# Linear attention, then a Mamba chain: GpSimd's share of the step product made uneven, its output sum, statistics, denominator and step products moved

## The chip, the cores and the metric

The kernel runs on one core of a Trainium2 chip. The core has TensorE (PE in the profile; PEld is its weight load), VectorE (DVE), ScalarE (ACT), GpSimd (POOL) and SyncE (SP, which only issues DMAs here). They run side by side and wait for each other by semaphores. The metric is the device time of one execution in microseconds, as the median of several runs.

## The reference

The input x has 8 samples of 512 channels and 2304 positions. Layer 0 is a group norm followed by causal linear attention with 8 heads, added to x. Layer 1 is a group norm followed by a chain of four Mamba blocks of 128 channels, each fed with the result of the one before, added to x again.

```python
q, k = elu(Wq x)+1, elu(Wk x)+1
den = 1 / (einsum(q, cumsum(k)) + 1e-10)
out = causal(q, k, v) * den
...
# Mamba block: 256 inner channels, 16 states
delta = softplus(dt @ Wdt.T + bdt)
dA  = exp(delta * A)               # decay
dBu = delta * xs * B               # step product
h_t = dA_t * h_{t-1} + dBu_t       # scan along the positions
y   = sum over states (C * h) + xs * D
...
fused = w_local * x_i + w_global * max(x_i, x_m)   # goes into the next block
```

## The kernel before, in words

**Chunks, slots and passes.** A *chunk* is 384 positions of one Mamba block of one sample. A block has 6 chunks, which is one *pass*; 8 samples of 4 blocks make 32 passes and 192 chunks. Two samples (two `Stream`s) take turns, pass by pass. The 256 x 16 states of a chunk are laid out as 8 *slots* (`SLOTS`); a slot has 4 groups of 128 partitions and 384 positions. The loop `slot(k)` runs over 1536 slots, and it writes out by hand the order of work on every engine.

**One slot.** GpSimd multiplies B by delta times x for the last `TAIL` = 152 columns of each group (`last_product`, L879), and VectorE does so for the other 232 columns from a copy `Bp` of B in PSUM that ScalarE makes (`inputs` L863, `product` L890). GpSimd's part is put into the queue two slots ahead, VectorE's part one slot ahead; in slot 7 VectorE does the products of both slots 0 and 1 of the next chunk. ScalarE computes the decay factors into PSUM banks (L900). VectorE runs four scans (L910). GpSimd multiplies the states by C (`weigh`, L923), and TensorE sums them over the states into `yp` (`gather`, L937), which is queued a slot and a half later: `waiting` holds up to two gathers and one is taken out in the middle of each slot. Five buffers `u` hold the states of a slot.

**Beside the slots.** Each half slot, `beside` steps a list of generators: `chunk` (the attention of a later sample), `Job.prepare` (projection, convolution, Silu L758 to L763, step sizes: two matmuls L782 and Softplus L793, then dx L834 on GpSimd), `pass_on` (mixes a block's result into the next block's input, and adds the result to x on GpSimd for the output, L696) and `statistics` (group-norm statistics of a later sample's input, L253). A generator yields when it wants its next step: a pair of the half slot and the least distance to its step before, or a distance alone as text ("1"), and with it how many free PSUM banks it needs. Six banks (`BANKS`) are shared by the decay factors and all these steps. `first` is the half slot at which a chunk begins.

**Statistics.** A sample has 24 pieces of 384 positions. Before, they are taken one per `PERIOD` (16 half slots, one chunk), by both samples of a pair in the same 24 chunks or nearly so: two in a chunk for a while, and then none.

**The denominator.** `den` is a product of `pr` with a selector (L405); VectorE adds 1e-10 (L433), takes the reciprocal (L434), and ScalarE spreads it (L441). TensorE turns it (L445), VectorE multiplies q with it (L450).

**Group norms and the end of a pass.** The attention's input norm is applied by GpSimd in four steps per chunk (L324) of each sample's first pass; the second norm's statistics end with a group norm on VectorE (L190 to L211), once a pass. At the end of a pass VectorE computes the two mixing weights: L587, an exponential on ScalarE, L593 (adds 1 to two numbers) and L594 (their reciprocal).

Of the kernel before, what the change touches and what calls it, by code (L numbers as in the profile page):

```python
# [9 lines left out]
F32 = mybir.dt.float32  # L10
# [7 lines left out]
P = 128  # L18
T = 128
LC = 384  # L20
NI, NQ, NGR = 4, 4, 4
SLOTS = 8
TAIL = 152
BANKS = 6
DEPTH = 3
LEAD = 11
# [2 lines left out]
BEFORE, PERIOD, DENSE, FIRST = 61, 16, 11, -115  # L29
# [20 lines left out]
def attention_then_mamba_kernel(  # L50
# [12 lines left out]
    nc = tc.nc  # L63
    B, _, L = x.shape
    NS = 16
    NC = L // LC
    assert L % LC == 0 and LC % T == 0

    cpool = ctx.enter_context(tc.tile_pool(name="consts", bufs=1))
# [6 lines left out]
    psx = ctx.enter_context(tc.tile_pool(name="psx", bufs=1, space=PSUM))  # L76
# [4 lines left out]
    ident = cst[:, C_ID : C_ID + P]  # L81
# [4 lines left out]
    hsel = cst[:, C_SEL : C_SEL + 2]  # L86
# [28 lines left out]
    def load_scales():  # L115
# [3 lines left out]
        nc.scalar.activation(w_a, w_a, AF.Exp)  # L119
        nc.scalar.mul(w_a, w_a, -1.0)  # L120

    power = cpool.tile([P, 4], F32, name="power")
    nc.gpsimd.memset(power, -0.5)

# [100 lines left out]
    def statistics(b):  # L225

        xv = x[b].rearrange("(t p) l -> p t l", p=P)
        stats = small.tile([P, 4, NC, 6], F32, tag="stats_a", name=f"stats_a{b}", bufs=2)
        if b == 0:

            xs = []

            def load(c):
                t = mpool.tile([P, 4, 1 + LC], F32, tag="u", name=f"xs_{c}", bufs=5)[:, :, 0:LC]
                nc.sync.dma_start(out=t, in_=xv[:, :, c * LC : (c + 1) * LC])
                xs.append(t)

            for c in range(5):
                load(c)
            load_projections()  # L240
            for c in range(NC):
                for ct in range(4):
                    nc.vector.bn_stats(stats[:, ct, c, :], xs[c][:, ct, :])
                if c == 0:
                    load(5)
                    fetch(0)
        else:
            when = begins[b] + b % 2
            for i in range(4 * NC):
                yield (when - 4, 1) if b > 1 else "1", 0  # L250
                xs = piece(b, i)
                yield (when, 1) if b > 1 else "1", 0
                nc.vector.bn_stats(stats[:, i // NC, i % NC, :], xs)  # L253
                when += PERIOD
        norms[b] = yield from group_norm(stats, 4, f"a{b}", 2)

    def piece(b, i):
# [22 lines left out]
    def chunk(m):  # L280


        b, o, c = parts[m]
        n = f"{b}_{o}_{c}"
        bank = Banks()
        NT = LC // T
        cols, tile_rows = slice(c * LC, (c + 1) * LC), slice(o * P, (o + 1) * P)
        subs = [slice(i * T, (i + 1) * T) for i in range(NT)]
# [96 lines left out]
        pr = new("pr")  # L385
# [15 lines left out]
        yield at(12), 1  # L401
        both = bank()
        den = both[:, 0 : 2 * NT]
        for i in range(NT):
            nc.tensor.matmul(den[:, 2 * i : 2 * i + 2], pr[:, subs[i]], hsel, start=True, stop=True)  # L405
        more = NT if c + 1 < NC else NT - 1
        ds = both[:, LC - NT * 64 : LC].rearrange("p (i d) -> p i d", i=NT)
        place = range(NT + 1) if c % 2 == 0 else range(NT, -1, -1)
# [2 lines left out]
        if c:  # L411
# [4 lines left out]
                start=True,  # L416
                stop=False,
                skip_group_check=True,
            )
        for i in range(more):  # L420
            for j in range(i + 1):
                for h in heads_of:
# [4 lines left out]
                        start=c == 0 and j == 0,  # L427
                        stop=j == i,
                        skip_group_check=True,
                    )  # L430
        yield at(14), 0
        rd = small.tile([P, 2 * NT], F32, tag="rd", name=f"rd_{n}", bufs=1)
        nc.vector.tensor_scalar_add(rd, den, 1e-10)  # L433
        nc.vector.reciprocal(rd, rd)  # L434
        while read[0] < m:
            yield "1w", 0
        nc.scalar.copy(S[:, kept_states, :], ds[:, 0:more, :])
# [84 lines left out]
    class Stream:  # L522
# [55 lines left out]
        def pass_on(self):  # L578
# [78 lines left out]
            for c in range(NC):  # L657

                cols, icols = slice(c * LC, (c + 1) * LC), slice(3 + c * LC, 3 + (c + 1) * LC)
                if now is None:  # L660
                    first = 2 * self.jobs[self.block * NC + c].start
                    yield (first - 30, 1), 0
                    now = loads(c)
                    yield (first - 25, 1), 0 if old is None else 1
                else:
                    yield "1", 0 if old is None else 1
                fu, xb, xa = now
                now = None
                if not last:
                    normed = dict(bias=norm[:, 1, :], scale=norm[:, 0, :])  # L670
                if old is None:
                    nc.scalar.activation(xi[:, icols], xb, AF.Identity, **normed)
                else:
                    bank = Banks()
                    mixed = bank()[:, 0:LC]
                    more = len(factors) == 3
                    for i, src in enumerate((xi[:, icols], fu)):
                        nc.tensor.matmul(  # L678
                            mixed, mix[:, i, :], src, start=i == 0, stop=i == 1, skip_group_check=True
                        )  # L680
                    yield "1", 0
                    nc.scalar.copy(fu, mixed)
                    if more:
                        nc.tensor.matmul(
                            mixed, mix[:, 2, :], xb, start=False, stop=True, skip_group_check=True
                        )
                    yield "1", 0
                    if more:
                        nc.scalar.activation(
                            xi[:, icols], mixed, AF.Identity, bias=norm[:, 1, :]  # L690
                        )
                    elif not last:
                        nc.scalar.activation(xi[:, icols], xb, AF.Identity, **normed)
                    bank.free()
                    self.ready = c + 1
                    nc.gpsimd.tensor_tensor(xa, xa, fu, ALU.add)  # L696
                    save(out[old[0], old[1] * P : (old[1] + 1) * P, cols], xa)
                self.ready = c + 1
                if last and c + 1 < NC:
                    yield "3", 0  # L700
                    now = loads(c + 1)

    class Job:
# [6 lines left out]
        def prepare(self):  # L710
# [64 lines left out]
            bank.free()  # L775
            scr = dpool.tile([2 * NS, LC], F32, tag="scr", name=f"scr_{n}")
            save(scr, dbc[0 : 2 * NS, :])
            yield "1", 2
            vps = []
            for h in range(2):  # L780
                vp = bank()[:, 0:LC]
# [1 line left out]
                    vp, steps_w[32:41, s, h * P : (h + 1) * P], dbc[32:41, :], start=True, stop=True  # L783
                )
                vps.append(vp)
            while spreading:
                yield "1w", 0
            spreading.append(n)
            yield "1", 0
            delta = mpool.tile([P, 2, LC], F32, tag="delta", name=f"delta_{n}", bufs=1)  # L790
            ahead(DEPTH + 2)
            for h in range(2):
# [66 lines left out]

        def inputs(self, pair):  # L860

            self.Bp = psx.tile([P, 2, LC - TAIL], F32, tag="Bp", name=f"Bp_{self.n}_{pair}")
            nc.scalar.copy(self.Bp, self.B[pair % 2][:, :, 0 : LC - TAIL])  # L863

        def skip(self, h):

# [4 lines left out]

        def last_product(self, s):

            shape, cols = [P, NGR, TAIL], slice(LC - TAIL, LC)
            h, q = s // NQ, s % NQ
            u = mpool.tile([P, NGR, 1 + LC], F32, tag="u", name=f"u_{self.n}_{s}", bufs=5)
            if self.c:
                nc.scalar.copy(u[:, :, 0], self.state[:, h, q, :])
            nc.gpsimd.tensor_tensor(  # L879
                u[:, :, 1 + LC - TAIL :],  # L880
                self.B[q // 2][:, q % 2, cols].unsqueeze(1).to_broadcast(shape),
                self.dxr[h][:, :, cols],
                ALU.mult,
            )
            return u

        def product(self, s, u):

            shape, cols = [P, NGR, LC - TAIL], slice(0, LC - TAIL)
            nc.vector.tensor_mul(  # L890
                u[:, :, 1 : 1 + LC - TAIL],
                self.Bp[:, s % 2, :].unsqueeze(1).to_broadcast(shape),
                self.dxr[s // NQ][:, :, cols],
            )
# [156 lines left out]
    for b in counted:  # L1051
        first = times[parts.index((b, 0, 0))]
        begins[b] = (first - 20) // PERIOD * PERIOD - 4 * NC * PERIOD - 2 if b > 1 else first - 64

    def begin(latest):

# [19 lines left out]
    def beside(half):  # L1076

        half_no[0] = half
        flush(every=False)
        begin(half // 2 + LEAD)  # L1080

        for t in heads:
            if t.need is not None and t.early() and t.fits() and t.due():
                t.step()
        held = False
        for t in tasks + heads:
            while t.need is not None and t.due():
                if not t.fits() or held and t.need[1]:
                    held = held or t.need[1] > len(spare)
                    break  # L1090
                t.step()
        prune()
# [64 lines left out]
    def slot(k):  # L1157
# [6 lines left out]
        if s == 2 and before is not None and not before.closed:  # L1164
            before.gated(1)
            tasks.insert(0, Task(finale(before)))
        elif s == 6:
            job.gated(0)
        beside(2 * k)
        for i in range(4):  # L1170
            job.scan(s, i, us[k], decays.pop(0))
# [140 lines left out]
```

## Time and profile before

| what | value |
|---|---|
| median of 3 runs | 8173.76 us (8166.18 to 8179.68) |
| profiled execution | 8173.45 us, its span 8171.6 us |
| granted TensorE clock, mean | 0.945 |
| VectorE idle, all in all | 345.8 us, of it some 140 ahead of the first scan at 196.1 us |
| GpSimd idle | 424.3 us |
| HBM | 1318.23 MB read, 327.68 MB written |

The busy share of each engine is its busy time over the span. A line of a group gives the source line, the engine, the operation, what it writes and reads, the count, the busy time, the mean duration and the idle time of the engine just ahead of it with what ended that. A line of the order of time gives the start, the duration (of a row of equal instructions, their whole stretch), the engine, the line and the operation; in square brackets stands the idle time ahead of it and what ended it. Instructions that follow each other on VectorE overlap a little in these records: four scans of 935 ns take 3.49 us together.

### The profile page before, as it was taken

The page shows a single profiled execution, that of the slowest core. Times are in us where ns is not written, and L with a number is a line of the kernel's source. Part 1 is how long each engine was busy: PE and PEld are TensorE (multiplying, and loading weights), DVE is VectorE, ACT ScalarE, POOL GpSimd, SP SyncE. Part 2 cuts the span into 40 slices and gives each one's busy share as a digit, 9 for nine tenths or more (in the row PEclk, how much of TensorE's full clock was granted, in tenths as well). Part 3 has the DMA queues.
Part 4 walks back from the last instruction along what each step waited for, and adds up shares of the span by engine and source line. Part 5 has one row for each costly group of instructions (what it writes and reads, how often), then busy time and mean ns, then how long its engine had stood idle before and what let it go on. Part 6 is the DMA issues. An engine that isn't in the chain of part 4 may idle for free. (4 is left out here: it accounts for less than half of the span.)

```text
span 8171.6 us, 133449 instructions
## 1 busy us (share of the span) xinstructions
PE 7371.7 (90%) x39882; PEld 3532.8 (43%) x39882; DVE 7825.8 (96%) x10534; ACT 6974.3 (85%) x14914; POOL 7747.3 (95%) x3905
## 2 busy tenths in 40 slices
PE   8889999998899999999899999999988999999975
PEld 5444444444444444444444444444444444444421
DVE  3999999999999999999999999999999999999998
ACT  3888888888888888888888888888888888888876
POOL 2999999999999999999999999999999999999999
PEclk9999999999999999999999999999999999999977
DMA  6778888877787788887787788887877777777765
GB/s 199 191 189 207 210 209 212 212 199 210 200 209 204 205 212 212 207 210 201 205 216 205 200 208 209 214 211 195 212 204 204 204 204 200 204 203 199 193 172 148
DMA packets 1097351, 1655.02 MB, mean 203 GB/s; under 512 B 143913, under 2 KB 989353, under 8 KB 1096498
## 3 DMA queue, kind: packets, MB, share of 16 engines
q1 hardware_dynamic: 1096626, 1646.48, 77.8%
q8 instruction: 317, 5.19, 0.3%
q14 instruction: 408, 3.34, 0.1%
HBM read 1318.23 MB, written 327.68 MB: 201 GB/s over the span
## 5 line engine op out<-in xcount | busy, mean ns | idle before, releaser
L910 DVE TENSOR_TENSOR_SCAN u<-bank,u 128x385 f32<-128x385 f32 (+1 forms) x6144 | 5435.3, 935 | 101.6 <-ACT bank L900 101.1
L923 POOL TENSOR_TENSOR u<-u,C 128x1536 f32<-128x1536 f32 x1536 | 4894.4, 3187 | 245.4 <-DVE u L910 164.3
L900 ACT ACTIVATE bank<-dr,scales 128x385 f32<-128x385 f32 (+1 forms) x6144 | 3422.3, 579 | 617.5 <-DVE u L910 573.9
L879 POOL TENSOR_TENSOR u<-B,dxr 128x608 f32<-128x608 f32 x1536 | 2285.6, 1488 | 14.8 <-DMA B<-scr 14.8
L300 PE MATMUL bank<-xn,wq 128*128 128x384 f32 x4608 | 1862.0, 552 | 262.4 <-DVE u L910 215.6
L890 DVE TENSOR_TENSOR u<-Bp,dxr 128x928 f32<-128x928 f32 x1536 | 1682.9, 1096 | 14.9 <-DMA dxr<-xscr 7.7
L937 PE MATMUL yp<-u,cst 128*32 128x384 f32 x12288 | 1357.6, 514 | 259.7 <-POOL u L923 147.7
L300 PEld LDWEIGHTS bank<-xn,wq 128*128 128x128 f32 x4608 | 939.9, 212 | 1153.2 <-DVE u L910 360.5
L722 PE MATMUL bank<-xi,wk 128*128 128x384 f32 x3072 | 1102.4, 502 | 14.5 <-ACT xr L508 13.7
L722 PEld LDWEIGHTS bank<-xi,wk 128*128 128x128 f32 x3072 | 556.2, 191 | 568.2 <-ACT bank L900 77.3
L937 PEld LDWEIGHTS yp<-u,cst 128*32 128x32 f32 x12288 | 249.3, 109 | 904.3 <-issue 412.7
L312 ACT ACTIVATE ex<-bank,bqkv_sb 128x384 f32<-128x384 f32 x384 | 221.1, 576 | 337.0 <-PE bank L300 336.1
L900 ACT ACT_TABLE_LOAD x382 | 490.1, 1283 | 6.9
L863 ACT COPY Bp<-B 128x464 f32<-128x464 f32 x768 | 419.6, 546 | 25.7 <-DMA B<-scr 12.4
L834 POOL TENSOR_TENSOR dx<-delta,xs 128x384 f32<-128x384 f32 x384 | 385.9, 1005 | 21.6 <-ACT delta L793 21.6
L733 PE MATMUL bank<-xi,scales 128*128 128x384 f32 x768 | 325.4, 510 | 50.3 <-ACT xs L758 50.3
L955 PE MATMUL bank<-yz,scales 128*128 128x384 f32 x768 | 328.1, 534 | 37.7 <-DVE yz L949 32.8
L782 PE MATMUL bank<-dbc,steps_w 9*128 9x384 f32 x768 | 306.0, 518 | 21.8 <-DVE rd L433 12.3
L769 PE MATMUL bank<-xs,scales 128*40 128x384 f32 x768 | 285.0, 494 | 0.0
L498 PE MATMUL bank<-sm,v 128*64 128x128 f32 x2304 | 255.2, 300 | 0.0
L793 ACT ACT_TABLE_LOAD x192 | 246.3, 1283 | 3.5
L758 ACT ACT_TABLE_LOAD x192 | 246.3, 1283 | 3.5
(123 smaller groups left out, 8101.2 us busy)
## 6 DMA issues: line engine op xcount, KB each, us to landing
dr<-dscr SPq DMA_DIRECT2D x1536, 192.0 KB, 4.2
dxr<-xscr SPq DMA_DIRECT2D x1536, 192.0 KB, 4.9
xn<-xn SPq DMA_DIRECT2D x192, 768.0 KB, 5.4
B<-scr SPq DMA_DIRECT2D x1536, 96.0 KB, 4.2
C<-scr SPq DMA_DIRECT2D x1536, 96.0 KB, 2.7
dscr<-delta SPq DMA_DIRECT2D x192, 384.0 KB, 5.2
xscr<-dx SPq DMA_DIRECT2D x192, 384.0 KB, 2.9
xn<-in_x SPq DMA_DIRECT2D x48, 768.0 KB, 5.3
```

What stands on the lines that cost most here:

```text
L300: nc.tensor.matmul(ps, wqs[m // NC][:, kt, j * P : (j + 1) * P], xn[:, kt, :], start=(kt == 0), stop=(kt == 3),)
L722: nc.tensor.matmul(xc, wk[:, k, h * P : (h + 1) * P], xi[:, c0 + k : c0 + k + LC], start=(k == 0), stop=(k == 3),)
L733: nc.tensor.matmul(zp, w_gate[:, s, h * P : (h + 1) * P], xi[:, c0 + 3 : c0 + 3 + LC], start=True, stop=True,)
L834: nc.gpsimd.tensor_tensor(dx[:, h, :], delta[:, h, :], xs[:, h, :], ALU.mult)
L863: nc.scalar.copy(self.Bp, self.B[pair % 2][:, :, 0 : LC - TAIL])
L879: nc.gpsimd.tensor_tensor(u[:, :, 1 + LC - TAIL :], self.B[q // 2][:, q % 2, cols].unsqueeze(1).to_broadcast(shape), self.dxr[h][:, :, col ...
L890: nc.vector.tensor_mul(u[:, :, 1 : 1 + LC - TAIL], self.Bp[:, s % 2, :].unsqueeze(1).to_broadcast(shape), self.dxr[s // NQ][:, :, cols],)
L900: nc.scalar.activation(dA[:, cols], self.dr[h][:, g, cols], AF.Exp, scale=w_a[:, self.w[1], NGR * h + g, q : q + 1],)
L910: nc.vector.tensor_tensor_scan(u[:, g, cols], dA[:, cols], u[:, g, cols], 0.0, ALU.mult, ALU.add,)
L923: nc.gpsimd.tensor_tensor(u[:, :, 0:LC], u[:, :, 1:], self.C[q // 2][:, q % 2, :].unsqueeze(1).to_broadcast([P, NGR, LC]), ALU.mult,)
L937: nc.tensor.matmul(self.yp[g * 32 : g * 32 + 32, 0:LC], state_sum, u[:, g, 0:LC], start=False, stop=s % NQ == NQ - 1, skip_group_check=True,)
L955: nc.tensor.matmul(self.xm[:, 0:LC], w_out[:, self.w[1], h, :], self.yz[:, h, :], start=(h == 0), stop=(h == 1),)
```

## The change

GpSimd's share of a step product becomes 128 columns in slots 0 and 1 of a chunk (`WIDE`) and 165 in slots 2 to 7 (`TAIL`); `Bp` takes the other 256 or 219. For samples 4 and later a piece of statistics is taken every second period, beginning earlier, so that a pair of samples takes one a chunk. The denominator's 1e-10 is added by TensorE, which starts the accumulation with a product of the unit matrix and a constant tile. The GpSimd add of the output (L696) waits for half slot `first - 17`, the second half of slot 7 of the chunk before the one ahead. The two step matmuls (L782) are issued in the step of Softplus, half a slot later than before. And in slot 1 the gather of slot 7 of the chunk before is issued at the slot's start and not in its middle.

In the order of the queues this reads so. On VectorE only the widths, the missing add and the places of the statistics differ. On GpSimd the output add stands between the last product with B and the last product with C of a chunk. On ScalarE the order is the same. On TensorE the gather of slot 7 now stands ahead of the step matmuls, and a small matmul ahead of `den`.

```diff
-TAIL = 152
+WIDE, TAIL = 128, 165
...
+    tiny = cpool.tile([P, 2 * LC // T], F32, name="tiny")
+    nc.gpsimd.memset(tiny, 1e-10)
...
-            when = begins[b] + b % 2
+            when, gap = begins[b] + (b % 2 if b < 4 else 0), PERIOD if b < 4 else 2 * PERIOD
...
-                when += PERIOD
+                when += gap
...
+        nc.tensor.matmul(den, ident, tiny, start=True, stop=False, skip_group_check=True)
         for i in range(NT):
-            nc.tensor.matmul(den[:, 2 * i : 2 * i + 2], pr[:, subs[i]], hsel, start=True, stop=True)
+            nc.tensor.matmul(
+                den[:, 2 * i : 2 * i + 2],
+                pr[:, subs[i]],
+                hsel,
+                start=False,
+                stop=True,
+                skip_group_check=True,
+            )
...
-        nc.vector.tensor_scalar_add(rd, den, 1e-10)
-        nc.vector.reciprocal(rd, rd)
+        nc.vector.reciprocal(rd, den)
...
+                    yield (first - 17, 1) if not last else "1", 0
                     nc.gpsimd.tensor_tensor(xa, xa, fu, ALU.add)
...
             save(scr, dbc[0 : 2 * NS, :])
-            yield "1", 2
+            while spreading:
+                yield "1w", 0
+            spreading.append(n)
+            yield "2", 2
             vps = []
...
                 vps.append(vp)
-            while spreading:
-                yield "1w", 0
-            spreading.append(n)
-            yield "1", 0
             delta = mpool.tile([P, 2, LC], F32, tag="delta", name=f"delta_{n}", bufs=1)
...
-            self.Bp = psx.tile([P, 2, LC - TAIL], F32, tag="Bp", name=f"Bp_{self.n}_{pair}")
-            nc.scalar.copy(self.Bp, self.B[pair % 2][:, :, 0 : LC - TAIL])
+            width = LC - (TAIL if pair else WIDE)
+            Bp = psx.tile([P, 512], F32, tag="Bp", name=f"Bp_{self.n}_{pair}")
+            self.Bp = Bp[:, 0 : 2 * width].rearrange("p (f l) -> p f l", f=2)
+            nc.scalar.copy(self.Bp, self.B[pair % 2][:, :, 0:width])
...
+            tail = TAIL if s > 1 else WIDE
+            shape, cols = [P, NGR, tail], slice(LC - tail, LC)
...
+            width = LC - (TAIL if s > 1 else WIDE)
+            shape, cols = [P, NGR, width], slice(0, width)
...
         begins[b] = (first - 20) // PERIOD * PERIOD - 4 * NC * PERIOD - 2 if b > 1 else first - 64
+        if b > 3:
+            begins[b] -= (4 * NC - b % 2) * PERIOD
...
+        if s == 1 and len(waiting) > 1:
+            waiting.pop(0)()
         beside(2 * k)
```

## The prediction on record

> **What bounds the kernel now.** I read the table of busy time first, then the groups, then the waits of VectorE, then the order of time inside one chunk (eight slots).
>
> ```profile
> PE 7371.7 (90%) x39882; PEld 3532.8 (43%) x39882; DVE 7825.8 (96%) x10534; ACT 6974.3 (85%) x14914; POOL 7747.3 (95%) x3905
> ...
> L910 DVE TENSOR_TENSOR_SCAN u<-bank,u 128x385 f32<-128x385 f32 (+1 forms) x6144 | 5435.3, 935 | 101.6 <-ACT bank L900 101.1
> L923 POOL TENSOR_TENSOR u<-u,C 128x1536 f32<-128x1536 f32 x1536 | 4894.4, 3187 | 245.4 <-DVE u L910 164.3
> L879 POOL TENSOR_TENSOR u<-B,dxr 128x608 f32<-128x608 f32 x1536 | 2285.6, 1488 | 14.8 <-DMA B<-scr 14.8
> L890 DVE TENSOR_TENSOR u<-Bp,dxr 128x928 f32<-128x928 f32 x1536 | 1682.9, 1096 | 14.9 <-DMA dxr<-xscr 7.7
> ```
>
> VectorE and GpSimd are both full; a scan waits for its decay factor (L900) 131 times, 101 us. Where that wait lies shows in the order of time, at the end of a chunk (VectorE, then ScalarE, then GpSimd):
>
> ```profile
> 2521.35 1.09 DVE L890 TENSOR_TENSOR u<-Bp,dxr 128x928 f32<-128x928 f32 x1
> 2522.37 1.79 DVE L910 TENSOR_TENSOR_SCAN u<-bank,u 128x385 f32<-128x385 f32 x2
> 2524.09 1.09 DVE L890 TENSOR_TENSOR u<-Bp,dxr 128x928 f32<-128x928 f32 x1
> 2525.10 0.54 DVE L512 BATCH_NORM_STATS2 stats_m<-xr 128x6 f32<-128x384 f32 x1
> 2525.57 0.93 DVE L910 TENSOR_TENSOR_SCAN u<-bank,u 128x385 f32<-128x385 f32 x1
> 2527.37 2.66 DVE L910 TENSOR_TENSOR_SCAN u<-bank,u 128x385 f32<-128x385 f32 x3 [0.87 <-ACT bank L900]
> ```
> ```profile
> 2521.47 0.59 ACT L900 ACTIVATE bank<-dr,scales 128x385 f32<-128x385 f32 x1 [0.27 <-DVE u L910]
> 2522.07 1.28 ACT L758 ACT_TABLE_LOAD   x1
> ...
> 2526.75 1.09 ACT L900 ACTIVATE bank<-dr,scales 128x385 f32<-128x385 f32 x2
> ```
> ```profile
> 2526.08 1.48 POOL L879 TENSOR_TENSOR u<-B,dxr 128x608 f32<-128x608 f32 x1
> 2528.47 3.17 POOL L923 TENSOR_TENSOR u<-u,C 128x1536 f32<-128x1536 f32 x1 [0.91 <-DVE u L910]
> ```
>
> In slot 7 ScalarE does the four Silu with two table loads; the last scan of the slot can't start before 2527.37, about 6.0 us after slot 6 ended (2521.35). In those 6.0 us VectorE idles 0.87 and GpSimd, held up by the late scan, 0.91. Everywhere else in this chunk VectorE runs back to back. Counting the scan starts by 32 gives each chunk's length: 53 of 192 last 40.4 us, whether they hold no statistic, one (wait 0.41) or two (wait 0): statistics lie in the hole and are free. So a chunk is a fixed window of 6.0 plus 34.4 us of VectorE work.
>
> **Part by part.** *The shares.* Slots 2 to 7 move 13 columns times 4 groups from VectorE to GpSimd. VectorE's price per element, from L890 (928: 1096 ns) and the 384-element product L386 (541 ns), is 555/544 = 1.02 ns: 52 elements are 53 ns, six products 0.32 us. All six lie in the 34.4 us, on the path. Slots 0 and 1 move 24 columns back: 96 elements, 98 ns each; both products lie in the window (2521.35 and 2524.09), where 0.87 us of waiting (0.41 with one statistic) covers them; without that cover they cost 0.2. GpSimd: L923 against its 384-element product (3187, 1005 ns) gives 1.89 ns an element, L879 against the same 2.16; so +0.10 to 0.11 in six slots, -0.18 to -0.21 in two: +0.23 us a chunk. Its chunk is 40.4 minus 0.9 idle, 39.5 of work, then 39.7.
>
> *The denominator.* VectorE loses the add L433: 141 ns and 30 ns to the dependent step, 0.17 us on the path. The reciprocal now reads PSUM. The Trainium skill (Perfetto Trace Analysis, Optimizing Scalar/DVE Operations) puts access at about 60 ns on SBUF and 125 on PSUM, which would leave 0.10. The rows: L433 read PSUM in 141 ns, L434 SBUF in 192, so PSUM isn't dearer here. I take 0.17; the rule would cost 144 x 0.07 = 10 us. Below nothing it can't go. TensorE gains a small matmul; the nearest row, L405, takes 0.83 us for six records, so 0.28 for two. The reciprocal has 0.8 us of slack after L423.
>
> *Output sum.* GpSimd's add L696 (1.0 us, 186 times) moves from slot 4 to just ahead of slot 7's product with C, into the 0.91 us hole. Nothing but that product is queued right behind it; the gather and the next chunk wait for that. Its store moves along on SP, past the loads of the next chunk's rows; only the buffer's next use, two chunks on, waits for it. With it there GpSimd has 0.1 to 0.2 us left (39.7 against 39.9).
>
> *Gather and step products.* The gather of slot 7 goes half a slot forward, ahead of the two step products (L782). Now L782 (1.55 us) runs 2529.86 to 2531.42, then the gather at 2531.70, when GpSimd lets it. Afterwards: gather to 2532.55, L782 to 2534.1. Softplus (L793) starts at 2534.70 after a table load that waits for nothing: 0.6 us of cover. Behind L782 stands the q projection L300 (2533.93 now, 1.38 of it waiting for a bank): 0.15 later. Price nothing, unless the product with C is late: then each us beyond 0.6 is ScalarE's.
>
> *Statistics.* One a chunk in the window instead of two or none: free either way; it keeps the cover above open from sample 4 on. For about 20 chunks with two (samples 2, 3) the two wider products cost 0.2.
>
> **Sum.** A free chunk (no normalization, no group norm in it) gains 0.32 + 0.17 = 0.49; the next bounds (GpSimd 39.7, TensorE's last 0.1) let me take 0.46. Of 192 chunks, 36 carry the attention's normalization on GpSimd (four L324 more): GpSimd is the bound there and they lose 0.23, as do 8 at the end: +10. Of the rest 24 hold a group norm and have TensorE without a gap from the projection on: gain 0. About 20 gain 0.29 (-6), 100 gain 0.46 (-46): -52 + 10 = -42. One stretch is still missing:
>
> ```profile
> 2461.72 3.19 POOL L923 TENSOR_TENSOR u<-u,C 128x1536 f32<-128x1536 f32 x1
> 2464.85 1.01 POOL L834 TENSOR_TENSOR dx<-delta,xs 128x384 f32<-128x384 f32 x1
> ```
> ```profile
> 2464.56 0.38 DVE L593 TENSOR_SCALAR wt<-wt 128x2 f32<-128x2 f32 x1
> ```
> ```profile
> 2464.97 0.17 DVE L594 RECIPROCAL wt<-wt 128x2 f32<-128x2 f32 x1
> ```
>
> L593, once a pass, adds 1 to two numbers; it ends with GpSimd's running instruction (2464.91). The median is 382 ns, but 5 of 32 took 2.8 to 5.8 us: they waited through that instruction and two or three behind it, until GpSimd stood idle. The change brings VectorE here 0.33 us earlier (add and three products) and GpSimd 0.3 later (three longer products): L593 meets the product 1.0 us before its end. The Trainium skill (SBUF — State Buffer, Who interferes with whom) says whoever starts first holds the shared port pair for the whole instruction: 0.65 us more, and for some 21 passes 14 us. The five rows speak for more: to GpSimd's idle moment, 3.4 us, so 3.0 more and 63 us in all. I take the rule's value, as 26 of the other waits ended with the first instruction, but not confidently: those met it 0.4 us or less before its end. Below nothing is excluded: L593 isn't removed.
>
> Forecast: -42 + 14 = -28 from the profiled execution's 8173.45 (span 8171.6; median of the runs 8173.76, the same): 8145.
>
> **Rivals.** *The port (slower).* L593 is held to the idle moment at 21 passes: -42 + 63 = +21, 8194. For: one met the product 0.9 us ahead of its end and took 3.31. Against: 26 didn't. It decides from about 2.0 us a pass on. *TensorE or GpSimd becomes the bound.* TensorE idles only 2.1 to 3.9 us a chunk, and some 1.6 is a fixed wait for the gather; with 0.28 more work and the steps behind the gather, free chunks gain 0.2 instead of 0.46: -26 off the 100, so 8145 + 26 = 8171. *All of it, and the port costs nothing* (L593 meets a gap): 8131, and 8120 if the group-norm chunks gain 0.46 too.
>
> **How the numbers follow.** Forecast 0.38, full gain 0.15, new bound 0.17, port 0.30. A measurement tells about 0.2%, 16 us. Forecast and full gain are faster: 0.53; new bound and a fifth of the port's chance are within: 0.23; the rest of the port's is slower: 0.24. The range runs from the full gain with the GpSimd-bound chunks' loss taken away (8110) to the port's case with a few passes more (8202).
>
> **What would show it.** Right: free chunks of 39.95 us; the slot-7 wait 0.67 without a statistic, 0.2 with one; L890 near 1043 and 1194 ns; L879 near 1590 and 1300; no POOL wait of 0.9 ahead of slot 7's product; L593's mean near 1.5 us. Wrong: L593 near 3.4 us (port), free chunks at 40.2 with L793 or L300 waiting behind L782 (new bound), or a scan waiting for L900 in slot 2, where it has 0.3 us to spare.

## The result and the profile after

The changed kernel takes 8202.53 us (median of 5 runs, 8191.29 to 8213.21) against 8169.36 us (8162.39 to 8179.68) for the kernel before on the same chip: 1.0039 times as long, 95% interval 1.0028 to 1.0051. That is 33 us slower, where 28 us less was forecast. The profiled execution has a span of 8196.9 us (before 8171.6), at a mean granted clock of 0.943 (before 0.945).

The page's busy times and the four groups shown before, after the change (L910 is now L923, L923 is L936, L879 is L891, L890 is L903):

```profile
PE 7431.8 (91%) x40266; PEld 3598.0 (44%) x40266; DVE 7798.2 (95%) x10342; ACT 6950.1 (85%) x14914; POOL 7802.0 (95%) x3906
...
L923 DVE TENSOR_TENSOR_SCAN u<-bank,u 128x385 f32<-128x385 f32 (+1 forms) x6144 | 5435.6, 935 | 125.9 <-ACT bank L913 75.4
L936 POOL TENSOR_TENSOR u<-u,C 128x1536 f32<-128x1536 f32 x1536 | 4896.0, 3188 | 204.6 <-DVE u L923 107.7
...
L891 POOL TENSOR_TENSOR u<-B,dxr 128x660 f32<-128x660 f32 (+1 forms) x1536 | 2341.6, 1524 | 22.2 <-DMA B<-scr 21.9
...
L903 DVE TENSOR_TENSOR u<-Bp,dxr 128x876 f32<-128x876 f32 (+1 forms) x1536 | 1659.3, 1080 | 14.1 <-ACT Bp L874 7.2
```

VectorE is busy 27.6 us less and GpSimd 54.7 us more, and the scans' wait for the decay factor fell from 101.1 to 75.4 us. So the work moved as planned, and yet the end came later. The end of a chunk looks as forecast too. VectorE, in order of time, at slot 7 of one chunk, then GpSimd:

```profile
2535.03 0.54 DVE L521 BATCH_NORM_STATS2 stats_m<-xr 128x6 f32<-128x384 f32 x1
2535.49 0.93 DVE L923 TENSOR_TENSOR_SCAN u<-bank,u 128x385 f32<-128x385 f32 x1
2536.64 2.66 DVE L923 TENSOR_TENSOR_SCAN u<-bank,u 128x385 f32<-128x385 f32 x3 [0.21 <-ACT bank L913]
```
```profile
2537.74 3.18 POOL L936 TENSOR_TENSOR u<-u,C 128x1536 f32<-128x1536 f32 x1
```

The wait is 0.21 us with one statistic (forecast 0.2), and GpSimd no longer idles ahead of slot 7's product with C. Free chunks last 39.89 us (forecast 39.95; before 40.41).

One wait that grew is one that the forecast did not touch: VectorE's multiplication of q with the transposed reciprocal. The line gives the total, the number of times and the longest wait; first before, then after:

```profile
DVE q L450 <- PE bank L445: 44.5, 59, 5.9
```
```profile
DVE q L459 <- PE bank L454: 87.9, 94, 4.4
```

A second wait is as large and stands under another name. Scans of slot 2 waited 52 times in the 184 chunks between the two ends, 47.8 us in all, and never before the change. The profile puts most of that down to GpSimd, as in the first line below. But each of these scans starts within 0.2 us of the end of its own decay factor (L913), which ScalarE computes behind Softplus; and Softplus and its table load (both L802) now wait for the step products (L795), which they never did before:

```profile
DVE u L923 <- POOL u L891: 19.9, 28, 2.1
```
```profile
ACT delta L802 <- PE bank L795: 53.9, 74, 2.0
ACT L802 <- PE bank L795: 31.3, 30, 3.2
```

On TensorE the wait of the gathers for GpSimd's product with C grew likewise, before and after:

```profile
PE yp L937 <- POOL u L923: 147.7, 185, 5.3
```
```profile
PE yp L950 <- POOL u L936: 391.8, 204, 4.8
```

TensorE's order of time in two chunks of the changed kernel shows what happens. In the first one the granted clock stays at 1.00:

```profile
2501.09 0.85 PE L950 MATMUL yp<-u,cst 128*32 128x384 f32 x8 [1.55 <-POOL u L936]
2501.87 1.55 PE L795 MATMUL bank<-dbc,steps_w 9*128 9x384 f32 x4
2503.35 2.85 PE L302 MATMUL bank<-xn,wq 128*128 128x384 f32 x8
2506.04 0.49 PE L454 MATMUL bank<-cst,rdb 128*128 128x128 f32 x3
```

VectorE comes to L459 only at 2508.61, two microseconds after L454 is done. In the next chunk the same four rows run like this, and VectorE's row stands behind them:

```profile
2540.98 0.85 PE L950 MATMUL yp<-u,cst 128*32 128x384 f32 x8 [1.55 <-POOL u L936]
2541.76 2.31 PE L795 MATMUL bank<-dbc,steps_w 9*128 9x384 f32 x4
2544.01 5.43 PE L302 MATMUL bank<-xn,wq 128*128 128x384 f32 x8
2549.27 0.49 PE L454 MATMUL bank<-cst,rdb 128*128 128x128 f32 x3
```
```profile
2549.80 0.55 DVE L459 TENSOR_TENSOR q<-q,bank 128x384 f32<-128x384 f32 x1 [1.21 <-PE bank L454]
```

The table by stretches of that chunk (stretch, length, busy time and count of PE, PEld, DVE, ACT, POOL, then PEclk, DMA share, GB/s) names the reason in its PEclk column:

```profile
2537.50:2540.90 3.40, 1.92 (x34) 0.94 (x32) 3.40 (x6) 3.40 (x10) 3.30 (x3) 1.00 0.66 186
...
2542.50:2549.30 6.80, 6.80 (x12) 3.12 (x11) 6.09 (x8) 5.23 (x10) 6.80 (x3) 0.50 1.05 293
```

For 6.8 us TensorE gets half its clock. The step products and the q projection, 4.40 us together in the first chunk, take 7.74.

The mean clock of the page hides this, for the records of the clock show it in many chunks and mostly in this place, for one or two pieces of 3.413 us: of the 120 stretches at half clock in the middle 184 chunks, 82 begin 3 to 6 us after slot 0 does. The kernel before has it too. I counted, in each kernel's one trace, the chunks (of 184, without those at the two ends) that hold at least two such pieces in their first 20 us, and call them *half-clock chunks* (such a count shifts by up to four with where the borders are drawn):

| kernel | half-clock chunks | their median | median of chunks with none |
|---|---|---|---|
| before | 79 | 41.35 us | 40.41 us |
| changed | 84 | 42.00 us | 39.89 us |

A chunk without it gained 0.52; one with it lost 0.65.

### The profile page after: what moved, and what is told of

It is laid out like the page before. It is cut to its first block, busy times and chain, and to the rows that moved or that the text cites. A ratio compares the mean times of both kernels' runs of the same rounds, so it can differ in the third digit from the quotient of the medians.

```text
span 8196.9 us, 133855 instructions
## 1 busy us (share of the span) xinstructions
PE 7431.8 (91%) x40266; PEld 3598.0 (44%) x40266; DVE 7798.2 (95%) x10342; ACT 6950.1 (85%) x14914; POOL 7802.0 (95%) x3906
## 5 line engine op out<-in xcount | busy, mean ns | idle before, releaser
L923 DVE TENSOR_TENSOR_SCAN u<-bank,u 128x385 f32<-128x385 f32 (+1 forms) x6144 | 5435.6, 935 | 125.9 <-ACT bank L913 75.4
L936 POOL TENSOR_TENSOR u<-u,C 128x1536 f32<-128x1536 f32 x1536 | 4896.0, 3188 | 204.6 <-DVE u L923 107.7
L913 ACT ACTIVATE bank<-dr,scales 128x385 f32<-128x385 f32 (+1 forms) x6144 | 3411.0, 579 | 544.5 <-DVE u L923 512.7
L891 POOL TENSOR_TENSOR u<-B,dxr 128x660 f32<-128x660 f32 (+1 forms) x1536 | 2341.6, 1524 | 22.2 <-DMA B<-scr 21.9
L903 DVE TENSOR_TENSOR u<-Bp,dxr 128x876 f32<-128x876 f32 (+1 forms) x1536 | 1659.3, 1080 | 14.1 <-ACT Bp L874 7.2
L874 ACT COPY Bp<-B 128x438 f32<-128x438 f32 (+1 forms) x768 | 414.9, 540 | 30.2 <-DVE u L903 15.9
L795 PE MATMUL bank<-dbc,steps_w 9*128 9x384 f32 x768 | 400.0, 653 | 1.9 <-ACT S L446 1.9
L795 PEld LDWEIGHTS bank<-dbc,steps_w 9*128 9x128 f32 x768 | 159.2, 228 | 212.4 <-ACT bank L913 99.3
```

The costliest lines, as they stand in the source:

```text
L795: nc.tensor.matmul(vp, steps_w[32:41, s, h * P : (h + 1) * P], dbc[32:41, :], start=True, stop=True)
L874: nc.scalar.copy(self.Bp, self.B[pair % 2][:, :, 0:width])
L891: nc.gpsimd.tensor_tensor(u[:, :, 1 + LC - tail :], self.B[q // 2][:, q % 2, cols].unsqueeze(1).to_broadcast(shape), self.dxr[h][:, :, col ...
L903: nc.vector.tensor_mul(u[:, :, 1 : 1 + width], self.Bp[:, s % 2, :].unsqueeze(1).to_broadcast(shape), self.dxr[s // NQ][:, :, cols],)
L913: nc.scalar.activation(dA[:, cols], self.dr[h][:, g, cols], AF.Exp, scale=w_a[:, self.w[1], NGR * h + g, q : q + 1],)
L923: nc.vector.tensor_tensor_scan(u[:, g, cols], dA[:, cols], u[:, g, cols], 0.0, ALU.mult, ALU.add,)
```

## The experiments

Ratios are to the kernel before on the same chip, with their 95% intervals.

**The order put back.** The first two tell whether TensorE's order is the cause.

```diff
-            while spreading:
-                yield "1w", 0
-            spreading.append(n)
-            yield "2", 2
+            yield "1", 2
             vps = []
...
+            while spreading:
+                yield "1w", 0
+            spreading.append(n)
+            yield "1", 0
             delta = ...
...
-        if s == 1 and len(waiting) > 1:
-            waiting.pop(0)()
         beside(2 * k)
```

> The changed kernel with the step products and the gather of slot 7 put back where they were (nothing else undone). Theory (TensorE's order): where the granted clock falls to 0.5 just as the late gather, the step products and the q projection follow each other, they take about twice as long and VectorE waits 1.2 us for the transposed reciprocal; undone, the chunks with such a dip come back from 42.0 to about 41.0 us, free chunks stay at 39.9, and the whole is 8135 to 8155. Rival (GpSimd's longer shares are the bound): nothing changes, 8195 to 8205. Rival (the port, L593): nothing changes either.

Measured: 8134.12 us (0.9956, 0.9944 to 0.9969). The order alone made 68 us of difference. Its trace has 60 half-clock chunks with a median of 41.14 us, and no scan of slot 2 waits. By the page's span and busy time VectorE idles 329.5 us, against 398.7 in the changed kernel. I compared the two traces chunk by chunk: the 53 chunks that hold two pieces at half clock only with the order of the change are 79 us longer there, and the 36 that hold none in either trace are not longer (6 us shorter in all). VectorE's wait, and TensorE's rows in one half-clock chunk (line numbers differ by a few: L792 are the step products, L951 the gather):

```profile
DVE q L459 <- PE bank L454: 49.7, 52, 4.4
```
```profile
2434.29 1.55 PE L792 MATMUL bank<-dbc,steps_w 9*128 9x384 f32 x4
2436.19 0.85 PE L951 MATMUL yp<-u,cst 128*32 128x384 f32 x8 [0.35 <-POOL u L937]
2437.87 5.49 PE L302 MATMUL bank<-xn,wq 128*128 128x384 f32 x8 [0.82 <-DVE u L924]
2443.15 0.85 PE L454 MATMUL bank<-cst,rdb 128*128 128x128 f32 x3
```
```profile
2444.04 0.56 DVE L459 TENSOR_TENSOR q<-q,bank 128x384 f32<-128x384 f32 x1 [0.54 <-PE bank L454]
```

Here the step products run at full clock while GpSimd still works on slot 7; only the q projection meets the half clock, and it starts 5.4 us into the chunk where it was 6.5 in the changed kernel. VectorE waits 0.54 us and not 1.21. Either half of this edit alone leaves TensorE's order as it was before: the step products and the gather only change places if both are moved.

**The order alone,** put into the kernel before (the same edit, the other way round).

> The kernel before with only the step products half a slot later and the gather of slot 7 ahead of them. Theory (TensorE's order): free chunks stay at 40.4 us, chunks with a clock dip at the end go from 41.5 to about 42.3, the whole 8210 to 8235. Rival (GpSimd's shares or the port): as before, 8165 to 8175.

Measured: 8205.56 us (1.0043, 1.0029 to 1.0057), 35 us slower; 84 half-clock chunks with a median of 42.29 us, free chunks unchanged at 40.41. The theory holds a little below its numbers. The rivals fall.

**The shares put back** (`WIDE, TAIL = 152, 152` in the changed kernel).

> The changed kernel with GpSimd's share back at 152 columns in all slots. Theory (TensorE's order): the loss stays and the gain of 0.32 us a free chunk goes, 8205 to 8230. Rival (GpSimd is the bound with its 0.23 us more a chunk): 8170 or less. Rival (the port): VectorE comes 0.3 us later and GpSimd 0.3 earlier to L593, whose mean goes back to 0.8 us: 10 us less of the loss, 8190.

Measured: 8193.26 us (1.0028, 1.0016 to 1.0039), within the intervals the same as the changed kernel. The number is the port rival's, and L602's mean did fall to 0.75 us; L602 takes 14.6 us less in all, which is worth some 10 us if each of them costs 0.7, as a later run finds for the changed kernel (an estimate: 27 for 38.7). The theory missed its range: free chunks are 0.33 us longer (40.22), as it said, but this trace also has fewer half-clock chunks (72 and not 84), and the scans of slot 2 wait 26.2 us and not 47.8. What each of these three is worth was not separated. GpSimd was not the bound.

**The add put back** (the small matmul out, `tensor_scalar_add` in).

> The changed kernel with the small matmul taken out and the add of 1e-10 back on VectorE. Theory (TensorE's order with a slow clock): VectorE does 0.17 us more in the free chunks, TensorE 0.28 less, but half a chunk away from the queue that is late: 8205 to 8220. Rival (TensorE's extra work in the normalization is what makes it late and pulls the clock down): 8180 or less, with fewer stretches at half clock than 134.

Measured: 8231.21 us (1.0075, 1.0062 to 1.0088), beyond both: more half-clock chunks (99), not fewer. TensorE's added matmul is not what slows it.

**Half of the q projection left out,** with the order of the change.

```diff
-            for kt in range(4):
+            steps = 4 if j else 2
+            for kt in range(steps):
```

> The changed kernel, with the order of the change kept, but the q projection of each attention chunk leaves out half of its sum (two of four matmuls). Theory (TensorE is late only because it does the late gather, the step products and the q projection one after another, at half clock in many chunks): with 1.4 us (2.7 at half clock) less in that row, the transposed reciprocal is in time again, the chunks with a dip come down from 42.0 to 41.2 us or less and the whole to 8110 to 8160. Rival (what the new order makes late is ScalarE's Softplus or the banks, not TensorE's own time): 8185 to 8205.

Measured: 8138.01 us (0.9961, 0.9948 to 0.9973). VectorE's wait for the transposed reciprocal is all but gone:

```profile
DVE q L460 <- PE bank L455: 6.4, 4, 3.1
```

So TensorE's own time in that row is what came late there. The rival holds for the other wait: the scans of slot 2, behind Softplus, still wait 59.0 us. At the same time the clock was worse (0.928, 94 half-clock chunks): less work made more half clock.

**The add of 1 as a sum of two tensors,** from here on with the order put back, to take away the hold of L602.

```diff
-                nc.vector.tensor_scalar_add(wt[:, 0:2], wt[:, 0:2], 1.0)
+                nc.vector.tensor_tensor(wt[:, 0:2], wt[:, 0:2], ones, ALU.add)
```

> The kernel of the first experiment (the order put back, all else of the change kept), with the add of 1 to two numbers (L602) done as an addition of two tensors on the same engine at the same place. In the first experiment its 32 calls took 51.8 us in all. Theory (they wait for the port that GpSimd holds, and that wait is on VectorE's path): they take about 0.1 us each, and the whole falls by 25 to 48 us from 8134, to 8086 to 8109. Rival (the wait is covered by what comes late behind it anyway, or the addition of two tensors waits too): 8125 to 8140.

Measured: 8138.68 us (0.9965, 0.9951 to 0.9979). It took nothing away: this form waited just as long, 51.6 us in all against 51.8. The lines give least, median and longest of the 32 calls in ns; before, the changed kernel, and this one (L604):

```profile
L593 DVE TENSOR_SCALAR wt<-wt x32: 169/382/5765, 462.9 to 8157.6; 128x2 f32<-128x2 f32 x32
```
```profile
L602 DVE TENSOR_SCALAR wt<-wt x32: 169/934/4130, 464.4 to 8182.6; 128x2 f32<-128x2 f32 x32
```
```profile
L604 DVE TENSOR_TENSOR wt<-wt,ones x32: 160/1074/5927, 455.4 to 8114.8; 128x2 f32<-128x2 f32 x32
```

The Trainium skill (SBUF — State Buffer, Who interferes with whom) has the reason: a VectorE instruction with two inputs in SBUF also meets GpSimd's reads, and this one has two. L903, which runs beside GpSimd throughout, has one of its inputs in PSUM.

**The shares put back, the order put back.**

> The kernel of the first experiment (the order put back), with GpSimd's share back at 152 columns in all slots. Theory (the shares gain 0.32 us in free chunks, cost 0.2 in those that GpSimd bounds, and bring L602 later into GpSimd's product, 51.8 us in all against about 24): free chunks 40.3, the whole 8128 to 8150. Rival (the shares gain their 0.32 us nearly everywhere and the port costs nothing): 8165 to 8185.

Measured: 8137.52 us (0.9962, 0.9950 to 0.9975), against 0.9956 with the new shares: no difference. Free chunks are 40.22 (39.99); L602 takes 39.6 us in all, not 24 as I had expected.

**The add put back, the order put back.**

> The kernel of the first experiment (the order put back), with the small matmul taken out and the add of 1e-10 back on VectorE. Theory (0.17 us of VectorE in some 140 chunks): 8150 to 8165. Rival (a reciprocal that reads PSUM is dearer by as much as the add was): 8130 to 8140.

Measured: 8161.34 us (0.9992, 0.9984 to 1.0000). The denominator's change is worth some 29 us. Not all of that need be VectorE's add: this trace has 77 half-clock chunks and not 60, and in the 30 chunks without half clock in both traces the median gain is 0.10 us (0.20 in the 34 such chunks with the order kept). L443, the reciprocal that reads PSUM, takes 170 ns; here, reading what the add just wrote to SBUF, it takes 192.

**The add of 1 on ScalarE,** where all 32 calls took 203 to 206 ns; and the same with the old shares.

```diff
                 nc.scalar.activation(wt[:, 0:2], wt[:, 2:4], AF.Exp, scale=-1.0 / L)
+                nc.scalar.activation(wt[:, 0:2], wt[:, 0:2], AF.Identity, bias=1.0)
                 yield "1", 0
-                nc.vector.tensor_scalar_add(wt[:, 0:2], wt[:, 0:2], 1.0)
```

> The kernel of the first experiment (the order put back) with the add of 1 to two numbers (L602) done by ScalarE right behind its Exp; VectorE keeps only the reciprocal, which took 0.17 us each time. The form tried before (a sum of two tensors in SBUF) was held just like L602, so it took nothing away; this form can't be held. Theory (the hold, 51.8 us in all, lies on VectorE's path): 8090 to 8112. Rival (what comes late behind it, GpSimd or TensorE, sets the end of that chunk anyway): 8128 to 8140.

> As the run before it (order put back, add of 1 on ScalarE), with GpSimd's share back at 152 columns in all slots. It completes a square with the first experiment and the one with the shares back. Theory (the wider shares gain 0.32 us in free chunks and lost it again to the held L602, 12 us, and in chunks that GpSimd bounds): without the hold the old shares are 10 to 25 us slower than the new ones, 8105 to 8130. Rival (GpSimd takes back all of the shares' gain, with or without the hold): the same time as the run before it, within 6 us.

Measured: 8076.55 us (0.9889, 0.9876 to 0.9903) and 8102.30 us (0.9922, 0.9909 to 0.9936). The hold was wholly on VectorE's path: 55 us by the ratios, for 51.8 us of L602. Without it the new shares are 26 us faster than the old ones. The hold had taken nearly all of that.

**The output sum put back, the statistics put back,** each with the order put back.

> The kernel of the first experiment (the order put back) with the output sum back in slot 4 (nothing else). Theory (its 1.0 us fills the hole ahead of slot 7's product with C; in slot 4 it comes on top of GpSimd's 39.7 us, so that a chunk can't be shorter than about 40.6): 8150 to 8180. Rival (GpSimd is not the limit, wherever the sum stands): 8128 to 8142.

> The kernel of the first experiment (the order put back) with two statistics a chunk in half of the chunks and none in the others, as before the change. Theory (they lie in the wait of slot 7; with two there is no cover left for the wider products, 0.2 us in some 60 chunks): 8136 to 8152. Rival (a statistic is on the path, or its loads hold up others): 8155 or more; rival (one statistic in every chunk is what makes them late): 8120 or less.

Measured: 8128.00 us (0.9956, 0.9943 to 0.9968), the same, so the theory fell and GpSimd isn't the limit there; and 8143.77 us (0.9971, 0.9961 to 0.9981), within the theory, but its interval meets that of the first experiment.

**The add of 1 on ScalarE in the changed kernel, and in the kernel before.**

> The changed kernel as it is, its order kept, with only the add of 1 to two numbers (L602, 38.7 us in all, 9.0 more than before the change) done by ScalarE. Theory (two separate costs: the order's some 60 to 80 us and the hold's, about 1.1 times what L602 took): 8202 falls by 35 to 50, to 8152 to 8168, and the order still costs 70 or more against the kernel with the order put back and the add on ScalarE (8077). Rival (in the changed kernel TensorE is late anyway and hides the hold): 8190 to 8205.

> The kernel before with only the add of 1 to two numbers (L593, 29.7 us in all) done by ScalarE. Theory (the hold is on VectorE's path, about 1.1 times its sum): 8169 falls to 8133 to 8145; the difference between the two runs of this call is then 10 to 15 us below that between the changed kernel and the kernel before, which is the hold's part of the result. Rival (before the change the hold was hidden): 8160 to 8170, and the hold's part is all of L602's 40 us.

Measured: 8176.02 us (1.0006, 0.9997 to 1.0015) and 8146.85 us (0.9969, 0.9958 to 0.9980). The hold costs 27 us in the changed kernel and 25 in the one before: it explains some 2 us of the 33, though the intervals leave room for some 15 us either way. Where TensorE is in time it costs twice that. The order costs 96 us once the hold is gone (1.0006 against 0.9889).

**The hole filled.** Why does the clock halve? In the changed kernel's trace all stretches at half clock begin on one grid of 3.413 us. Of its pieces in which TensorE was busy less than half of the time, 60 of 66 were followed by half clock (34 of 45 with the order put back); of the 433 between, 58; of those busy over 90%, none of 1743. The Trainium skill (TensorE: Matmul & The Clock Gate, What's actually happening) says that the clock follows how busy TensorE was in a free-running window of 3413 ns, which is this grid. By it, an idle window halves the clock; the windows here were partly busy. The order of the change leaves TensorE idle ahead of the late gather, in most chunks for some 1.55 us.

Whether such a hole halves the clock depends on where it lies. In the two chunks shown above the piece of the grid around the hole was busy 1.86 us of 3.41, yet the clock fell only behind the second: there the hole ended 2.0 us after a grid point, in the first 3.0. The changed kernel's trace has 110 holes of 1.4 to 1.7 us in this place at full clock. All 37 that were followed by half clock at the next grid point ended 0.3 to 2.3 us after a grid point, and only two of the other 73 did. (Of 61 longer ones, 58 were followed by it.) So the same code, with the same hole, runs at full clock in one chunk and at half in the next.

The next kernels keep that order and compute something there to throw away.

```diff
             spreading.append(n)
-            yield "2", 2
+            yield "1", 1
+            twice = bank()[:, 0:LC]
+            for h in range(2):
+                nc.tensor.matmul(
+                    twice, steps_w[32:41, s, h * P : (h + 1) * P], dbc[32:41, :], start=True, stop=True
+                )
+            bank.free()
+            yield "1", 2
```

> The changed kernel, its order kept, with the two step products computed once more, into a bank that is thrown away, in the hole that the order leaves TensorE ahead of the gather of slot 7 (1.55 us of added work a chunk; the needed ones follow behind the gather as before). In the trace of the changed kernel every stretch at half clock begins on one grid of 3.413 us, behind a piece of that grid in which TensorE was busy 0.48 of the time on average; behind pieces busy over 0.9 of the time none of 1743. Theory (the hole pulls the clock down, and the order puts the work behind it): more work, but fewer chunks with two pieces at half clock (84 now, 40 to 65 then), and the whole 8130 to 8185. Rival (TensorE simply has too much to do one after another in that place): 8200 to 8230, with as many such chunks as now.

Measured: 8216.31 us (1.0066, 1.0052 to 1.0080), 69 half-clock chunks. The theory fell in this form: TensorE is recorded as busy, and the clock halves nearly as often, now also behind 36 of the 1878 pieces that were busy over 90%. So busy time as recorded isn't all that counts. The step products use 9 rows; the next kernel fills the hole with products of 128.

```diff
-                    twice, steps_w[32:41, s, h * P : (h + 1) * P], dbc[32:41, :], start=True, stop=True
+                    twice, ident, xs[:, h, :], start=True, stop=True
```

> As the run before it (the hole ahead of the late gather filled, the result of the filler thrown away), but the filler is two products of the identity with the 128 rows of x instead of the step products, which use 9 of TensorE's 128 rows. Theory (what counts for the clock is how much of TensorE is at work, and 9 rows count for little): fewer than 60 chunks with two pieces at half clock, against 69 in the run before it and 84 in the changed kernel, and 8130 to 8195. Rival (the filler's rows make no difference; the clock follows something else): 65 or more such chunks, 8205 to 8230.

Measured: 8126.86 us (0.9953, 0.9939 to 0.9967), 12 half-clock chunks. The same 1.56 us of filler, with 128 rows and not 9, makes the kernel 70 us faster than the changed one, although TensorE does more, and 92 us faster than the 9-row filler, with which it shares the order, the banks and the length. The data differ with the rows, so the rows alone were not tested. Chunk by chunk against the changed kernel, the 74 chunks that held two pieces at half clock and now hold at most one are 97 us shorter, and the 72 that hold none in either trace are 2 us longer in all. The mean clock of its core, and the rows of one chunk (L794 is the filler, L957 the gather, L802 the step products):

```profile
core 0: 8109.5 us, clock 0.978
```
```profile
2514.24 1.56 PE L794 MATMUL bank<-xs,cst 128*128 128x384 f32 x4
2515.86 0.85 PE L957 MATMUL yp<-u,cst 128*32 128x384 f32 x8
2516.65 1.55 PE L802 MATMUL bank<-dbc,steps_w 9*128 9x384 f32 x4
2518.13 2.85 PE L302 MATMUL bank<-xn,wq 128*128 128x384 f32 x8
```

The order is the changed kernel's, and with the filler the kernel is as fast as with the order put back (0.9953 and 0.9956). That is a balance, for the clock is better here than there (0.978 and 0.945 in the traces), and 16.4 us of the wait in slot 2 are left.

**Together.**

> The changed kernel with its order, the 128-row filler in the hole and the add of 1 on ScalarE. Theory (the hold of L602, 26 us in the changed kernel and 58 where TensorE was not late, comes off in full now that TensorE is in time): 8068 to 8100. Rival (the hold is worth 26 as in the changed kernel): 8100 to 8105; rival (what the filler gave was the same time as the hold's): 8120 or more.

> The order put back, the add of 1 on ScalarE (8077 so far), and the 128-row filler ahead of the step products. Theory (the filler keeps the clock up in the 51 chunks that still had two pieces at half clock, each some 1.2 us longer; it delays the gather by about 1.2 us, which the later wait for a bank covers): 8020 to 8065. Rival (1.5 us more of TensorE's time costs as much as the clock gives back): 8070 to 8095.

Measured: 8073.88 us (0.9885, 0.9871 to 0.9899), as the theory said, and with 0.9889 of the version with the order put back the fastest here: 1.1% less than before the change. The second took 9130.06 us (1.1172, 1.1154 to 1.1190), which none had expected. The filler's bank shifted the ring: the q projection now got the bank that the step products held, and TensorE waited 609.7 us, in 180 places, for Softplus to read it. So the old order with the clock kept up is not measured.

## Why the prediction was wrong

**The step that failed** is that of the gather and the step products: "Price nothing, unless the product with C is late". Its working took all durations from a chunk at full clock: step products 1.55 us, then the q projection 0.15 us later. It was right for that chunk (L454 is done two microseconds ahead of its reader) and wrong for the 84 in which the clock halves behind the hole. In the one shown the step products take 2.31 us, the q projection starts 1.1 us later than in the other order, and VectorE waits 1.21 us. The 0.6 us of cover for Softplus failed too: it waited for L795 104 times, 85.2 us in all, most of them in the same chunks, and 30 times already with its table load, which the forecast took to wait for nothing. The decay factors behind it then came late for the scans of slot 2, by 47.8 us. The step measured +68 us against the order put back, +35 in the kernel before, and +96 without the hold. In chunks at full clock it costs nothing, as forecast, and a filler that keeps the clock up takes the whole loss away: the reasoning missed the clock. Part of the wait in slot 2 may be what the forecast set apart as "unless the product with C is late", for 16.4 us of it stay with the filler. What exactly the clock's control counts is not shown.

**The rest of the sum held in part by luck.** Without the order the change gives -36 us (0.9956), against a forecast of -28. But two misses cancel in that. With the add of 1 on ScalarE in both, the change without its order gives -65 us (0.9889 against 0.9969, some 14 us either way), where the forecast had -42 for these parts; so the hold costs some 30 us more there than before, where it had 14. Why the parts give more than their sum was not tried; the traces with the small matmul also have fewer half-clock chunks. The free chunks, the slot-7 wait, the narrower and the wider products (1.04 and 1.19 us in the trace) and GpSimd's two durations (1.61 and 1.28) are as forecast. The reciprocal from PSUM is not dearer: 170 ns. The PSUM price of the Trainium skill (Perfetto Trace Analysis, Optimizing Scalar/DVE Operations) that the prediction weighed would have left 0.10 of the 0.17 us; the rows of the two reciprocals (170 and 192 ns) show no such price, but the 29 us of the edit can't tell 0.10 from 0.17, since half-clock chunks changed with it.

**L602 (L593 before)** mostly behaved as the rule said: 13 calls ended with GpSimd's running instruction at 0.92 to 0.96 us, and six waited 3.4 to 4.1. So the port rival fell in its size. Its calls took 9 us more in all, and its part of the result comes out at some 2 us, where 14 was forecast; the intervals are too wide to tell these apart. What the forecast missed is that the hold was a cost worth removing all along.

**The output sum** was said to fit the hole. It does, but it cost nothing in slot 4 either (0.9956 both ways with the order put back); why not, no run tells.

**Rivals.** The one on TensorE was nearest: it named the steps behind the gather, and two of the signs came, L802 waiting behind L795 and a scan waiting for its decay factor in slot 2. But it looked for the loss in the free chunks (40.2 us), which gained in full.

## What to carry to other kernels

Before a step is moved in TensorE's queue, look at the granted clock in the stretch that it moves into, not at the mean: a row that fits at full clock may be the late one at half. A hole in TensorE's queue can be paid twice, by the wait and by the clock behind it; try work that uses all 128 rows in it, needed or not, and look which bank it takes (the same filler gained 70 us in one order, and in the other the kernel lost some 1050). And look for short VectorE instructions that read SBUF and last longer than their size: moving 32 additions of two numbers to ScalarE gave 55 us with the order put back, where the shifting of shares gave 26.

## What the runs showed of the hardware

- TensorE's clock halves in a kernel that has it busy 91% of the time: 941 us of 8196.9 in the changed kernel, all on one grid of 3.413 us. In the same hole, a filler on 9 rows did not keep it up (930 us at half clock), one on 128 rows mostly did (361 us).
- A hole of 1.4 to 1.7 us was followed by half clock in 37 of 110 cases, and its place on the grid told which: all 37 ended 0.3 to 2.3 us after a grid point, as did only two of the others.
- The kernels with the old order and the small matmul have 39 to 60 half-clock chunks; those with the old order and the add on VectorE 77 to 85; those with the new order and no filler 72 to 99. Each is one trace, and why the small matmul should matter wasn't tried.
- An instruction of VectorE that meets GpSimd's reads is mostly let in when GpSimd's running instruction ends, but in 5 of 32 calls before the change and 6 to 8 in the changed kernel and with the order put back only two or three GpSimd instructions later (2.8 to 6.4 us). What decides that stays open.
